# Products with W1 by Strassen-Winograd on pairs of row tiles, laid between the next steps' matmuls

## The chip, the cores and the metric

The kernel runs on one core of one Trainium2 chip. The metric is the device time in microseconds (us), the median over repeated executions. All data is fp32.

## What is computed

There are 3327 rows (26 tiles of 128, the last one padded) with 512 columns; `adj` is 3327 x 3327. With h = relu(layernorm(x)):

```python
# layer 0: attention, a bias of twice the adjacency
q = h @ Wq.T + bq;  k = h @ Wk.T + bk;  v = h @ Wv.T + bv
a = q @ k.T * scale + adj + adj
x = x + softmax(a) @ v
# layer 1: normalised graph convolution, h made again from the new x
A2 = adj + eye;  d = diagonal(A2) ** -0.5
temp = A2 @ h @ W1.T
x = x + relu((d[:, None] * A2 * d[None, :]) @ temp)
```

The products with W1 that the title speaks of are `(A2 @ h) @ W1.T`, 26 tiles of 128 x 512 by 512 x 512, each scaled by d.

## The kernel before

After the scores (lines up to about 570) the kernel does three large products one after the other, which the code numbers g = 0, 1, 2: softmax weights times h, A2 times h, A2 times temp. Each is a 2 x 2 Winograd scheme of seven products, taken in the order `ORDER` = p5, p1, p6, p7, p2, p3, p4. Each of the seven is done for two strips of output columns (s = 0, 896 wide, and s = 1, 768 wide), and each of these is a second Winograd level along the 13 row tiles: six steps t = 0 to 5 of a pair of tiles, seven matmuls each into seven PSUM banks, and one step t = None for the thirteenth tile, four matmuls. There are 294 steps; step k = ((g * 7 + place in ORDER) * 2 + s) * 7 + t. A matmul of a step has 448 columns for s = 0 and 384 for s = 1.

`run(k)` writes the instructions of step k for all engines, in an order that is kept on each engine (`in_order` covers VectorE, TensorE, GpSimd, ScalarE and SyncE):

- SyncE: `load` of step k + 3, the left operand (L701), into a ring of five slots.
- TensorE: the seven matmuls (L782), or the four of t = None (L774).
- VectorE, after them: the sums of the left operand of step k + 2 (`sums`, with `four_sums`, L173 to L175, and additions on the diagonal, L764), into a ring of three slots.
- At t = 5, `Gather.first` (L810 to L814) reads four of the seven banks. At t = None, `Gather.rest` (L827 to L830) reads the other three and one more, and `Gather.settle` (L836 to L843) puts the result into the output regions `cts`. The next step, t = 0, starts over in the same banks.
- Last, what the table `between` lists for step k: `Right.load` for a right operand five steps ahead (L721), `Right.make` three steps ahead (L742 to L748 and `four_differences`, L180 to L183), and row work.

Row work follows a product once the rows of its output are complete. For g = 0 it is `attend`. For g = 1 it is `temp(i)`, one row tile in each step from k = 177 on, leaving out the steps t = None, to k = 206: four matmuls of 512 columns with W1 into bank 3 (L874, `times_weights`), a multiplication by d on ScalarE (L902), a store through GpSimd (L903). The rows are stored in DRAM and loaded back as the right operand of g = 2. For g = 2 it is `finish`: four transposes (L927), relu (L929), the addition of x (L930) and the store (L92); the x comes by `finish_load`, which ScalarE issues (L910) at the end of the step before. In the table `within`, other `finish` calls come after the fourth matmul of a step.

Of the kernel before, what the change touches and what calls it, by code (L numbers as in the profile page):

```python
# [10 lines left out]
F32 = mybir.dt.float32  # L11
AF = mybir.ActivationFunctionType
ALU = mybir.AluOpType
AX = mybir.AxisListType

P = 128
# [20 lines left out]
PAIRS = 6  # L37
# [6 lines left out]
ROW = tuple(STRIPS[s] + y * HT[s] + k for y in range(2) for s in range(2) for k in range(HT[s]))  # L44
# [3 lines left out]
def graph_layers_kernel(  # L48
# [54 lines left out]
    def mid(k, shape, name):  # L103
        return arena.tile(shape, F32, name=name, tag=f"mid{k}")

    def half(k, shape, name):
        return arena.tile(shape, F32, name=name, tag=f"half{k}")

    def bank(k, name):
        return banks.tile([P, BW], F32, name=name, tag=f"bank{k}")  # L110

    def ring(*slots):

        turn = itertools.cycle(slots)
# [23 lines left out]
    const = ctx.enter_context(tc.tile_pool(name="const", bufs=1))  # L138
# [31 lines left out]

    def four_sums(o, g):

        nc.vector.tensor_add(o[:, 0:2], g[:, 0:4:3], g[:, 1:2].to_broadcast([P, 2, g.shape[-1]]))  # L173
        nc.vector.tensor_add(o[:, 2], o[:, 1], g[:, 0])  # L174
        nc.vector.tensor_add(o[:, 3], o[:, 2], g[:, 2])  # L175

    def four_differences(b, first=0):

        if first == 0:
            yield nc.vector.tensor_sub(b[4], b[0], b[1])  # L180
        yield nc.vector.tensor_add(b[5], b[3], b[4])
        yield nc.vector.tensor_sub(b[6], b[1], b[3])
        yield nc.vector.tensor_sub(b[7], b[2], b[5])  # L183
# [47 lines left out]
    class Chain:  # L231
# [320 lines left out]
    with in_order(*(e.engine for e in (nc.vector, nc.tensor, nc.gpsimd, nc.sync))):  # L552
# [9 lines left out]
        k = len(steps)  # L562
# [75 lines left out]
    def prepared():  # L638
        nc.vector.reciprocal(rs, tot)
        nc.vector.tensor_scalar(dg, dg, 1.0, None, op0=ALU.add)  # L640
        nc.gpsimd.tensor_tensor(sd, dg, mh, op=ALU.pow)

    wv_w1 = []

    def other_weights():
        wv_w1.append(weights(w1T))


    parts = {}
# [27 lines left out]
    x_slots = [lambda k=k: view(2, 1).rearrange("p a w -> p (a w)")[:, k * D : (k + 1) * D] for k in range(3)]  # L677
    x_slots = itertools.cycle([*x_slots, lambda: mid(10, [P, D], "xt")])
    h_ring = ring((mid, 11))
    ts_ring = ring(*spare[:3])  # L680
    xr_ring = ring(*spare[:3], (half, 14))
    out_ring = ring((half, 12), (half, 13), *spare[3:])
    xr_last = ring(*((half, k) for k in (4, 5, 6)))
# [23 lines left out]
    class Right:  # L707
# [31 lines left out]
        def make(self):  # L739
            own, r = self.own, self.r  # L740
            if r == "p5":
                nc.vector.tensor_sub(own, self.two[:, :, 0:E], self.two[:, :, E:D])  # L742
            if r == "p6":
                nc.vector.tensor_add(own, own, self.two[:, :, 0:E])
                nc.vector.tensor_sub(own, own, self.two[:, :, E:D])
                nc.gpsimd.dma_start(self.t2[:, 0 : 2 * self.n], self.b[:, 0 : 2 * self.n])
            if r in ("p7", "p4"):
                nc.vector.tensor_sub(own, own, self.one)  # L748
            if self.n == 2:
                for _ in four_differences([self.b[:, k] for k in range(8)]):  # L750
                    pass

    class Step:

# [6 lines left out]

        def sums(self):
            for a, d in self.diagonals:
                nc.vector.tensor_add(a, a, d)  # L764
            if self.t is None:
                return
            self.o = o_ring3()[:, :, : Q[self.s]]
            four_sums(self.o, self.a.rearrange("p k y w -> p (k y) w"))

        def multiply(self, ps):  # L770
            a, b, w = self.a, self.right.b, Q[self.s]
# [15 lines left out]
    class Gather:  # L787
# [44 lines left out]
        def settle(self):  # L832
            r11, r12, r21, r22 = self.regions
            for k, to in enumerate(self.to):
                if self.r == "p6":
                    nc.vector.tensor_sub(r12[k], to, r11[k])  # L836
                elif self.r == "p7":
                    nc.vector.tensor_add(r21[k], to, r12[k])
                    nc.vector.tensor_sub(r12[k], r22[k], r12[k])
                    nc.vector.tensor_sub(r22[k], r21[k], r22[k])  # L840
                elif not self.place and not self.last:
                    t = {"p2": r11, "p3": r12, "p4": r21}[self.r]
                    nc.vector.tensor_add(t[k], t[k], to)  # L843

    def where(i):

# [23 lines left out]
    def times_weights(i, w):  # L870
        s, y, k = where(i)
        ps = bank(ROLE["p8"], "p8")
        for d in range(DC):
            nc.tensor.matmul(ps, cts[s][y][d][:, k * P : (k + 1) * P], w[d], start=d == 0, stop=d == DC - 1)  # L874
        return ps
# [19 lines left out]

    normed = {}

    def temp(i):

        ps = times_weights(i, wv_w1[1])  # L900
        ts = ts_ring([P, D], "ts")
        nc.scalar.mul(ts, ps, sd[:, i : i + 1])  # L902
        nc.gpsimd.dma_start(rowd[2][i], ts)  # L903

    xrs = {}

# [57 lines left out]
    def rows(g, k, i, *z):  # L964

        if g == 0:
            at(k - 2, attend_load, i)
            at(k, attend, i)
            at(k + 1, attended, i)
        elif g == 1:  # L970
            at(k, temp, i)
        else:
            at(k - 1, finish_load, i, *z)
            at(k, finish, i, *z)

    for g in range(2):
        k = number_of(g, 5, 1, 2)
        for i in ROW:  # L980
            if steps[k].t is None:
                k += 1
            rows(g, k, i)
            k += 1
    within = {}
    for (n, s, t), its in {
# [12 lines left out]
        at(number_of(2, 6, 1, 2) + n, last_load, i)  # L999
    for k, what in ((1, totals), (2, prepare), (6, prepared), (8, judge), (9, judged)):  # L1000
        at(k, what)
    at(number_of(1, 1, 0, 4), other_weights)

    for k in range(3):
        steps[k].load()
    for what in early:
        what()
    for k in range(2):
        steps[k].sums()
    banks_of, gathers = {}, {}  # L1010

    def run(k):
        step = steps[k]
        if k + 3 < len(steps):
            steps[k + 3].load()
        if step.t == 0:
            banks_of.update(seven())
        if not cts:
            set_up()
        if step.t is None:  # L1020
            banks_of["p8"] = bank(ROLE["p1"], "p8")
        t, sums = step.t, steps[k + 2].sums if k + 2 < len(steps) else tuple
        if t == PAIRS - 1:
            gathers[step.r, step.s] = Gather(step.r, step.s, k == len(steps) - 2)
        gatherer = gathers.get((step.r, step.s))
        for j, _ in enumerate(step.multiply(banks_of)):
            if j == 3 and t == PAIRS - 1 and gatherer.last:
                gatherer.first(banks_of)
            for what, args in within.get(k, ()) if j == 3 else ():
                what(*args)  # L1030
        if t is None:
            gatherer.rest(banks_of)
        sums()
        if t == PAIRS - 1 and not gatherer.last:
            gatherer.first(banks_of)
        if t is None:
            gatherer.settle()
        for what, args in between.get(k, ()):
            what(*args)

    with in_order(*(e.engine for e in (nc.vector, nc.tensor, nc.gpsimd, nc.scalar, nc.sync))):
        for k in range(len(steps)):
# [379 lines left out]
```

## Time and profile before

| | |
|---|---|
| median of 6 runs | 2211.89 us (2209.56 to 2215.72) |
| profiled execution, its own time | 2213.65 us |
| its span, first to last instruction | 2211.8 us |
| TensorE busy | 2178.4 us (98%) |
| VectorE busy | 1627.2 us (74%) |
| ScalarE busy | 230.9 us (10%) |
| mean granted TensorE clock | 0.995 |
| matmuls with W1 and Wv together (L874) | 416 records, 189.2 us |

In the profile PE is the matmul stream of TensorE and PEld its weight loads, DVE is VectorE, ACT ScalarE, POOL GpSimd, SPq and ACTq are DMA issues of SyncE and ScalarE. An fp32 matmul shows as two records, a transpose as one. A line of a timeline has start, length, engine, source line, operation, output<-input, shape and count, and in brackets the idle time before with what ended it. The length of a run of matmuls holds the tail of the last one, so the cost of one is read from the starts. A DVE entry's start-to-start distance can be smaller than its length.

### The profile page before, as it was taken

What the parts mean: (1) busy time and instruction counts of PE and PEld (TensorE: products, weight loads), DVE (VectorE), ACT (ScalarE), POOL (GpSimd) and SP (SyncE); (2) the same over time, 40 slices, a digit from 0 to 9 for tenths busy, and PEclk for the clock granted to TensorE, in tenths of its full rate; (3) what the DMA queues carried; (4) which work ended last, traced back from release to release, by engine and by line L of the source; (5) the groups of instructions that cost most, each with busy time, mean ns of one, the idle gap of its engine ahead of it and who ended that gap; (6) DMA issues with size and microseconds to landing.
All of it is one profiled execution on the core that took longest, in us unless ns stands there. A gap on an engine that the chain in (4) does not pass through costs nothing.

```text
span 2211.8 us, 20973 instructions
## 1 busy us (share of the span) xinstructions
PE 2178.4 (98%) x6268; PEld 1168.0 (53%) x6268; DVE 1627.2 (74%) x3103; ACT 230.9 (10%) x335; POOL 357.1 (16%) x551
## 2 busy tenths in 40 slices
PE   9999999999999999999999999999999999999997
PEld 6555555455545555555454555555545555555554
DVE  6369888888877788777777778886645358777776
ACT  5311121112110000000010000000000000000011
POOL 4223333333321000001222100000000000000001
PEclk9999999999999999999999999999999999999999
DMA  8568888888969898888797899876645458765684
GB/s 286 187 218 295 295 295 285 302 283 310 358 214 327 304 376 293 274 290 310 252 310 266 312 343 351 286 267 200 215 140 191 132 185 304 236 200 186 209 299 167
DMA packets 246682, 583.68 MB, mean 264 GB/s; under 512 B 34768, under 2 KB 106270, under 8 KB 246558
## 3 DMA queue, kind: packets, MB, share of 16 engines
q1 hardware_dynamic: 192270, 399.28, 54.1%
q0 software_dynamic: 44928, 167.49, 20.0%
q10 hardware_dynamic: 9360, 15.47, 2.1%
q8 instruction: 52, 0.85, 0.2%
q14 instruction: 72, 0.59, 0.1%
HBM read 414.28 MB, written 167.85 MB: 263 GB/s over the span
## 4 chain that ended last, share of the span: by engine, by line
PE 89%; DVE 4%; DMA 3%; issue 3%; POOL 1%; SPq 0%; ACT 0%; ACTq 0%; POOLq 0%; DVEq 0%
PE p L782 52%; PE Y L454 12%; PE p L874 7%; PE Z L454 6%; PE p L774 5%; PE X L454 3%; PE Y L347 1%; DMA b<-row 1%; DVE part L173 1%; PE mm L306 1%; DMA g<-in_adjT_dram 0%; PE pt L927 0%; DVE part L174 0%; PE Z L347 0%; DMA xr<-x1d 0%
## 5 line engine op out<-in xcount | busy, mean ns | idle before, releaser
L782 PE MATMUL p<-part,b 128*128 128x448 f32 (+1 forms) x3528 | 1255.3, 514 | 6.7 <-DVE part L174 4.9
L782 PEld LDWEIGHTS p<-part,b 128*128 128x128 f32 x3528 | 669.1, 190 | 572.2 <-issue 307.8
L173 DVE TENSOR_TENSOR part<-part 128x896 f32<-128x896 f32 (+1 forms) x252 | 256.9, 1020 | 96.7 <-PE p L782 41.4
L454 PE MATMUL Y<-qt,hp 128*128 128x448 f32 (+1 forms) x832 | 308.9, 514 | 2.4 <-DVE g L458 1.5
L454 PEld LDWEIGHTS Y<-qt,hp 128*128 128x128 f32 x832 | 157.0, 190 | 138.1 <-issue 72.3
L454 PE MATMUL Z<-qt,hp 128*128 128x384 f32 (+1 forms) x416 | 162.6, 513 | 0.0
L175 DVE TENSOR_TENSOR part<-part,part 128x448 f32<-128x448 f32 (+1 forms) x219 | 129.5, 591 | 16.9 <-DVE part L174 0.9
L174 DVE TENSOR_TENSOR part<-part,part 128x448 f32<-128x448 f32 (+1 forms) x219 | 129.4, 591 | 7.4
L774 PE MATMUL p<-part,b 128*128 128x448 f32 (+1 forms) x336 | 124.2, 513 | 0.0
L874 PE MATMUL p<-w,ct 128*128 128x512 f32 x272 | 123.5, 593 | 0.5 <-DVE part L886 0.5
L454 PEld LDWEIGHTS Z<-qt,hp 128*128 128x128 f32 x416 | 78.8, 190 | 67.4 <-issue 37.2
L458 DVE SCALAR_TENSOR_TENSOR g<-g,Y 128x384 f32<-128x384 f32 (+1 forms) x156 | 91.3, 585 | 28.4 <-PE Y L454 27.4
L868 POOL DMA_DIRECT2D sum<-job x52 | 28.4, 547 | 502.8 <-DVE job L865 287.0
L811 DVE TENSOR_TENSOR part<-p,part 128x384 f32<-128x384 f32 (+1 forms) x33 | 19.3, 586 | 107.2 <-PE p L782 106.5
L774 PEld LDWEIGHTS p<-part,b 128*128 128x128 f32 x336 | 63.6, 190 | 53.8 <-issue 32.6
L810 ACT COPY part<-p 128x384 f32<-128x384 f32 (+1 forms) x33 | 16.6, 502 | 685.5 <-PE p L782 684.6
L874 PEld LDWEIGHTS p<-w,ct 128*128 128x128 f32 x272 | 51.5, 190 | 59.6 <-issue 51.9
L454 PE MATMUL X<-qt,hp 128*128 128x384 f32 (+1 forms) x208 | 81.1, 512 | 0.0
L461 ACT ACTIVATE g<-g 128x768 f32<-128x768 f32 (+1 forms) x48 | 43.0, 896 | 352.4 <-DVE g L458 299.2
L446 POOL DMA_DIRECT2D sum<-o x52 | 36.8, 708 | 220.7 <-DVE o L440 152.1
L874 PE MATMUL p<-w,part 128*128 128x512 f32 x144 | 65.7, 592 | 0.0
L92 POOL DMA_DIRECT2D out_dram<-r x30 | 16.2, 541 | 304.3 <-DVE r L930 270.0
(165 smaller groups left out, 1880.5 us busy)
## 6 DMA issues: line engine op xcount, KB each, us to landing
part<-sum SPq DMA_DIRECT2D x104, 448.0 KB, 5.0
part<-p SPq DMA_DIRECT2D x91, 448.0 KB, 6.1
part<-sum SPq DMA_DIRECT2D x104, 384.0 KB, 3.5
part<-p SPq DMA_DIRECT2D x91, 384.0 KB, 4.3
part<-in_adjT_dram SPq DMA_DIRECT2D x78, 448.0 KB, 4.7
b<-row SPq DMA_DIRECT2D x234, 128.0 KB, 4.9
part<-in_adjT_dram SPq DMA_DIRECT2D x78, 384.0 KB, 3.7
g<-in_adjT_dram SPq DMA_DIRECT2D x52, 448.0 KB, 4.5
```

Source lines behind the costliest of these rows:

```text
L173: nc.vector.tensor_add(o[:, 0:2], g[:, 0:4:3], g[:, 1:2].to_broadcast([P, 2, g.shape[-1]]))
L174: nc.vector.tensor_add(o[:, 2], o[:, 1], g[:, 0])
L175: nc.vector.tensor_add(o[:, 3], o[:, 2], g[:, 2])
L306: nc.tensor.matmul(ps[r], w_q[c // 2][:, c % 2, r * P : (r + 1) * P], w_k[c // 2][:, c % 2], start=c == 0, stop=c == DC - 1)
L446: nc.gpsimd.dma_start(self.to(sumd)[:, 0:2], self.o)
L454: nc.tensor.matmul(ps[:, :wd], h_of(self.t, name, k), qt[B[name]][:, k], start=start and k == 0, stop=k == 1, skip_group_check=True)
L458: nc.vector.scalar_tensor_tensor(a[n], a[n], 2.0, ps[:, :wd], op0=ALU.mult, op1=ALU.add if sign > 0 else ALU.subtract)
L461: nc.scalar.activation(g[1], g[1], AF.Exp, **({"bias": pad} if self.t == HALF - 1 else {}))
L774: yield nc.tensor.matmul(ps[("p2", "p3", "p4", "p8")[k]][:, :w], b[:, z], a[:, 0, y], start=k == 3, stop=True)
L782: yield nc.tensor.matmul(ps[r][:, :w], b[:, i], m, start=self.t == 0, stop=self.t == PAIRS - 1 and r in ("p1", "p5", "p6", "p7"))
L868: nc.gpsimd.dma_start(sumd[self.s][self.j][:, 2 + self.k], self.a)
L874: nc.tensor.matmul(ps, cts[s][y][d][:, k * P : (k + 1) * P], w[d], start=d == 0, stop=d == DC - 1)
```

## The change

Two row tiles are taken together as a 2 x 2 block matrix (128 rows by 256 columns each) and multiplied with W1 as 2 x 2 blocks of 256 x 256 by Winograd's seven products. Each product is two matmuls of 256 columns into one half of bank 3. The 13 pairs start two steps apart. A pair's seven products are put between the matmuls of two steps: before the first and after the second, fourth and sixth matmul of one step, and after the first, third and fifth of the next.

ScalarE takes four of the seven results out of PSUM and VectorE three. VectorE makes four sums of the pair's blocks first (eight additions of 128 columns). W1's blocks come by four DMAs in step 154 instead of step 116; their four differences are made by VectorE in steps 157 to 160, and ScalarE turns a sign in step 162.

VectorE's functions become generators that yield after each instruction. In and before steps that hold such products, the work that stood after the matmuls of a step waits in a list, and two instructions of it follow each matmul of the next step. What is left of an older step is written at the end of the step. In all other steps it follows the matmuls as before. Every `between` entry with "load" in its name now comes before the step's matmuls, in every step.

```diff
     def four_sums(o, g):
-        nc.vector.tensor_add(o[:, 0:2], g[:, 0:4:3], g[:, 1:2].to_broadcast([P, 2, g.shape[-1]]))
...
+        yield nc.vector.tensor_add(o[:, 0:2], g[:, 0:4:3], g[:, 1:2].to_broadcast([P, 2, g.shape[-1]]))
...
     def other_weights():
-        wv_w1.append(weights(w1T))
+        b11, b21, b22, t1, t2, t3 = blocks((11, 12, 13), "w1")
+        b12, t4 = (mid(k, [P, 2, E], "w1") for k in (10, 11))
+        W.extend((b11, b12, b21, b22, t1, t2, t3, t4))
+        for z in range(2):
+            for y in range(2):
+                block = w1T[z * E : (z + 1) * E, y * E : (y + 1) * E]
+                nc.sync.dma_start(W[2 * z + y], block.rearrange("(c p) e -> p c e", p=P))
+        differences.append(four_differences(W))
...
-    def temp(i):
-        ps = times_weights(i, wv_w1[1])
-        ts = ts_ring([P, D], "ts")
-        nc.scalar.mul(ts, ps, sd[:, i : i + 1])
-        nc.gpsimd.dma_start(rowd[2][i], ts)
+    PARTS = (("p2", 1, True, 0, 1), ("m1", 0, True, 0, -1), ("p5", 1, False, 3, -1), ("p6", 0, False, 1, -1),
+             ("p3", 1, False, 1, 1), ("p7", 0, False, 3, 1), ("p4", 0, False, 2, 1))
+    AFTER = ((0, 0), (0, 2), (0, 4), (0, 6), (1, 1), (1, 3), (1, 5))
+    class Temp:
...
+        def sums(self):
+            a11, a12, a21, a22 = self.blocks()
+            self.o = half(14, [P, 4, 2, P], "rows")
+            for k, x, y in ((1, a21, a22), (2, None, a11), (3, None, a12), (0, a11, a21)):
+                for c in range(2):
+                    yield nc.vector.tensor_add(self.o[:, k, c], self.o[:, {2: 1, 3: 2}[k], c] if x is None else x[c], y[c])
+        def product(self, j):
+            name, h, new, n, sign = PARTS[j]
...
+            for c in range(2):
+                a = self.o[:, {"p7": 0, "p5": 1, "p6": 2, "p3": 3}[name], c] if left is None else self.blocks()[left][c]
+                nc.tensor.matmul(ps, a, W[B[name]][:, c], start=new and c == 0, stop=c == 1, skip_group_check=True)
...
+            if name in ("p2", "p5", "p6", "p4"):
+                nc.scalar.mul(to, ps, by)
+            else:
+                nc.vector.scalar_tensor_tensor(to, ps, by, to, op0=ALU.mult, op1=ALU.add)
...
     def run(k):
...
+        for what, args in between.get(k, ()):
+            if "load" in what.__name__:
+                what(*args)
...
+        weighs = any((k, j) in inserted for j in range(7))
+        if k in sums_of and not waiting:
+            do(sums_of.pop(k)())
+        for j, _ in enumerate(itertools.chain((None,), step.multiply(banks_of))):
+            for w, n in inserted.get((k, j), ()):
+                w.product(n)
...
+            if j == 2 and k in sums_of:
+                sums = sums_of.pop(k)()
+                do(sums, 4)
+                waiting.insert(1, sums)
+            elif weighs and j > 0:
+                do(first_of(waiting), 2)
         if t is None:
+            do(first_of(waiting))
             gatherer.rest(banks_of)
-        sums()
+        added = 2 + (t is None)
+        waiting.append(steps[k + 2].sums() if k + 2 < len(steps) else iter(()))
         if t == PAIRS - 1 and not gatherer.last:
+            do(first_of(waiting))
             gatherer.first(banks_of)
         if t is None:
-            gatherer.settle()
-        for what, args in between.get(k, ()):
-            what(*args)
+            waiting.append(gatherer.settle())
+        waiting.append(flow([(what, args) for what, args in between.get(k, ()) if "load" not in what.__name__]))
+        if (k + 1, 0) not in inserted and (k + 1, 1) not in inserted:
+            do(first_of(waiting))
+        while len(waiting) > added:
+            do(waiting.pop(0))
```

More of the change, by code (lines that the diff above doesn't have):

```diff
@@ L171, in four_sums @@
     def four_sums(o, g):
-        nc.vector.tensor_add(o[:, 0:2], g[:, 0:4:3], g[:, 1:2].to_broadcast([P, 2, g.shape[-1]]))
-        nc.vector.tensor_add(o[:, 2], o[:, 1], g[:, 0])
-        nc.vector.tensor_add(o[:, 3], o[:, 2], g[:, 2])
+        yield nc.vector.tensor_add(o[:, 0:2], g[:, 0:4:3], g[:, 1:2].to_broadcast([P, 2, g.shape[-1]]))
+        yield nc.vector.tensor_add(o[:, 2], o[:, 1], g[:, 0])
+        yield nc.vector.tensor_add(o[:, 3], o[:, 2], g[:, 2])
     def four_differences(b, first=0):
@@ L641, in prepared, with difference, turn_sign @@
         nc.gpsimd.tensor_tensor(sd, dg, mh, op=ALU.pow)
+        nc.scalar.mul(nsd, sd, -1.0)
     wv_w1 = []
+    W, differences = [], []
     def other_weights():
-        wv_w1.append(weights(w1T))
+        b11, b21, b22, t1, t2, t3 = blocks((11, 12, 13), "w1")
[6 more added lines that the diff above has]
+        differences.append(four_differences(W))
+    def difference():
+        next(differences[0])
+    def turn_sign():
+        nc.scalar.mul(W[0], W[0], -1.0)
+    nsd = const.tile([P, NT], F32, name="nsd")
     parts = {}
@@ L679, in graph_layers_kernel @@
     h_ring = ring((mid, 11))
-    ts_ring = ring(*spare[:3])
+    ts_slots = [lambda k=k: view(2, 1).rearrange("p a w -> p (a w)")[:, k * D : (k + 1) * D] for k in range(3)]
+    ts_slots = itertools.cycle([*ts_slots, *(lambda k=k: mid(k, [P, D], "ts") for k in range(12, 15))])
     xr_ring = ring(*spare[:3], (half, 14))
@@ L741, in make @@
             if r == "p5":
-                nc.vector.tensor_sub(own, self.two[:, :, 0:E], self.two[:, :, E:D])
+                yield nc.vector.tensor_sub(own, self.two[:, :, 0:E], self.two[:, :, E:D])
             if r == "p6":
-                nc.vector.tensor_add(own, own, self.two[:, :, 0:E])
-                nc.vector.tensor_sub(own, own, self.two[:, :, E:D])
+                yield nc.vector.tensor_add(own, own, self.two[:, :, 0:E])
+                yield nc.vector.tensor_sub(own, own, self.two[:, :, E:D])
                 nc.gpsimd.dma_start(self.t2[:, 0 : 2 * self.n], self.b[:, 0 : 2 * self.n])
             if r in ("p7", "p4"):
-                nc.vector.tensor_sub(own, own, self.one)
+                yield nc.vector.tensor_sub(own, own, self.one)
             if self.n == 2:
-                for _ in four_differences([self.b[:, k] for k in range(8)]):
-                    pass
+                yield from four_differences([self.b[:, k] for k in range(8)])
     class Step:
@@ L763, in sums @@
             for a, d in self.diagonals:
-                nc.vector.tensor_add(a, a, d)
+                yield nc.vector.tensor_add(a, a, d)
             if self.t is None:
@@ L767, in sums @@
             self.o = o_ring3()[:, :, : Q[self.s]]
-            four_sums(self.o, self.a.rearrange("p k y w -> p (k y) w"))
+            yield from four_sums(self.o, self.a.rearrange("p k y w -> p (k y) w"))
         def multiply(self, ps):
@@ L835, in settle @@
                 if self.r == "p6":
-                    nc.vector.tensor_sub(r12[k], to, r11[k])
+                    yield nc.vector.tensor_sub(r12[k], to, r11[k])
                 elif self.r == "p7":
-                    nc.vector.tensor_add(r21[k], to, r12[k])
-                    nc.vector.tensor_sub(r12[k], r22[k], r12[k])
-                    nc.vector.tensor_sub(r22[k], r21[k], r22[k])
+                    yield nc.vector.tensor_add(r21[k], to, r12[k])
+                    yield nc.vector.tensor_sub(r12[k], r22[k], r12[k])
+                    yield nc.vector.tensor_sub(r22[k], r21[k], r22[k])
                 elif not self.place and not self.last:
                     t = {"p2": r11, "p3": r12, "p4": r21}[self.r]
-                    nc.vector.tensor_add(t[k], t[k], to)
+                    yield nc.vector.tensor_add(t[k], t[k], to)
     def where(i):
@@ L896, in graph_layers_kernel, with __init__, blocks @@
     normed = {}
-    def temp(i):
-        ps = times_weights(i, wv_w1[1])
-        ts = ts_ring([P, D], "ts")
-        nc.scalar.mul(ts, ps, sd[:, i : i + 1])
-        nc.gpsimd.dma_start(rowd[2][i], ts)
+    PARTS = (("p2", 1, True, 0, 1), ("m1", 0, True, 0, -1), ("p5", 1, False, 3, -1), ("p6", 0, False, 1, -1),
+             ("p3", 1, False, 1, 1), ("p7", 0, False, 3, 1), ("p4", 0, False, 2, 1))
+    AFTER = ((0, 0), (0, 2), (0, 4), (0, 6), (1, 1), (1, 3), (1, 5))
+    class Temp:
+        def __init__(self, *its):
+            self.its = its
+        def blocks(self):
+            return [[cts[s][y][2 * z + c][:, k * P : (k + 1) * P] for c in range(2)]
+                    for s, y, k in map(where, self.its) for z in range(2)]
+        def sums(self):
[6 more added lines that the diff above has]
+            name, h, new, n, sign = PARTS[j]
+            if j == 0:
+                self.ps = bank(ROLE["p8"], "pw").rearrange("p (k e) -> p k e", k=2)
+                self.to = [next(ts_slots)() for _ in self.its]
+            left, ps = {"m1": 0, "p2": 1, "p4": 3}.get(name), self.ps[:, h]
+            for c in range(2):
+                a = self.o[:, {"p7": 0, "p5": 1, "p6": 2, "p3": 3}[name], c] if left is None else self.blocks()[left][c]
+                nc.tensor.matmul(ps, a, W[B[name]][:, c], start=new and c == 0, stop=c == 1, skip_group_check=True)
+            i = self.its[n // 2]
+            to, by = self.to[n // 2][:, n % 2 * E : (n % 2 + 1) * E], (sd if sign > 0 else nsd)[:, i : i + 1]
+            if name in ("p2", "p5", "p6", "p4"):
+                nc.scalar.mul(to, ps, by)
+            else:
+                nc.vector.scalar_tensor_tensor(to, ps, by, to, op0=ALU.mult, op1=ALU.add)
+            if j == len(PARTS) - 1:
+                for i, ts in zip(self.its, self.to):
+                    nc.gpsimd.dma_start(rowd[2][i], ts)
     xrs = {}
@@ L969, in rows @@
             at(k + 1, attended, i)
-        elif g == 1:
-            at(k, temp, i)
         else:
@@ L974, in rows @@
             at(k, finish, i, *z)
[L978 to L983, printed above, removed]
-            k += 1
+    k = number_of(0, 5, 1, 2)
+    for i in ROW:
+        if steps[k].t is None:
+            k += 1
+        rows(0, k, i)
+        k += 1
+    inserted, sums_of = {}, {}
+    k = number_of(1, 5, 1, 2)
+    for n in range(0, NT, 2):
+        if steps[k].t is None:
+            k += 1
+        w = Temp(*ROW[n : n + 2])
+        sums_of[k] = w.sums
+        for j, (later, m) in enumerate(AFTER):
+            inserted.setdefault((k + later, m), []).append((w, j))
+        k += 2
     within = {}
@@ L1001, in graph_layers_kernel @@
         at(k, what)
-    at(number_of(1, 1, 0, 4), other_weights)
+    k = number_of(1, 4, 0, 0)
+    at(k, other_weights)
+    for n in range(4):
+        at(k + 3 + n, difference)
+    at(k + 8, turn_sign)
     for k in range(3):
@@ L1006, in graph_layers_kernel, with flow, first_of, do @@
     for what in early:
-        what()
+        for _ in what() or ():
+            pass
     for k in range(2):
-        steps[k].sums()
+        for _ in steps[k].sums():
+            pass
     banks_of, gathers = {}, {}
+    waiting = []
+    def flow(tasks):
+        for what, args in tasks:
+            yield from what(*args) or (None,)
+    def first_of(parts):
+        while parts:
+            for _ in parts[0]:
+                yield
+            parts.pop(0)
+    def do(part, n=None):
+        for _ in itertools.islice(part, n):
+            pass
     def run(k):
@@ L1021, in run @@
             banks_of["p8"] = bank(ROLE["p1"], "p8")
-        t, sums = step.t, steps[k + 2].sums if k + 2 < len(steps) else tuple
+        t = step.t
+        for what, args in between.get(k, ()):
+            if "load" in what.__name__:
+                what(*args)
         if t == PAIRS - 1:
@@ L1025, in run @@
         gatherer = gathers.get((step.r, step.s))
-        for j, _ in enumerate(step.multiply(banks_of)):
-            if j == 3 and t == PAIRS - 1 and gatherer.last:
+        weighs = any((k, j) in inserted for j in range(7))
[4 more added lines that the diff above has]
+                w.product(n)
+            if j == 4 and t == PAIRS - 1 and gatherer.last:
                 gatherer.first(banks_of)
-            for what, args in within.get(k, ()) if j == 3 else ():
+            for what, args in within.get(k, ()) if j == 4 else ():
                 what(*args)
+            if j == 2 and k in sums_of:
[4 more added lines that the diff above has]
+                do(first_of(waiting), 2)
         if t is None:
+            do(first_of(waiting))
             gatherer.rest(banks_of)
-        sums()
+        added = 2 + (t is None)
+        waiting.append(steps[k + 2].sums() if k + 2 < len(steps) else iter(()))
         if t == PAIRS - 1 and not gatherer.last:
+            do(first_of(waiting))
             gatherer.first(banks_of)
         if t is None:
-            gatherer.settle()
-        for what, args in between.get(k, ()):
-            what(*args)
+            waiting.append(gatherer.settle())
[4 more added lines that the diff above has]
+            do(waiting.pop(0))
     with in_order(*(e.engine for e in (nc.vector, nc.tensor, nc.gpsimd, nc.scalar, nc.sync))):
```

## The prediction

> **What bounds the kernel now.** I read the busy times first, then the matmuls with W1 in the timeline, then what TensorE waits for, then VectorE where its work moves.
>
> ```profile
> PE 2178.4 (98%) x6268; PEld 1168.0 (53%) x6268; DVE 1627.2 (74%) x3103; ACT 230.9 (10%) x335; POOL 357.1 (16%) x551
> ```
>
> TensorE bounds the kernel: all that is idle is 33 us. A change pays if it shortens the matmul stream without opening gaps in it. From the timeline, first in the stage of `temp`, then early in the kernel among transposes:
>
> ```profile
> 1560.47 4.68 PE L782 MATMUL p<-part,b 128*128 128x384 f32 x14
> 1564.98 3.60 PE L874 MATMUL p<-w,ct 128*128 128x512 f32 x8
> 1565.41 0.19 PEld L874 LDWEIGHTS p<-w,ct 128*128 128x128 f32 x1 [0.24 <-issue]
> 1568.42 4.68 PE L782 MATMUL p<-part,b 128*128 128x384 f32 x14
> ...
> 50.45 0.60 PE L327 MATMUL tp<-ident,ht 128*128 128x128 f32 x4
> 50.88 0.81 PE L347 MATMUL Y<-hp,M 128*128 128x384 f32 x2
> ```
>
> From 1564.98 to 1568.42 eight records of 512 columns (one `temp`) take 3.44 us, 0.43 each; a step of 384 columns takes 4.51 (1560.47 to 1564.98). Four transposes of 128 columns take 0.43, 0.1075 each. So cost goes with columns, and weights load behind the matmul before. From 1550 to 1790 us TensorE's waits are empty: `temp` costs its full time today.
>
> Then VectorE around the end of a product (t = 5, None, 0):
>
> ```profile
> 1577.92 0.56 DVE L811 TENSOR_TENSOR part<-p,part 128x384 f32<-128x384 f32 x1 [12.19 <-PE p L782]
> ...
> 1580.20 0.68 DVE L748 TENSOR_TENSOR b<-b,rows 128x512 f32<-128x512 f32 x1
> ...
> 1585.16 0.56 DVE L827 TENSOR_TENSOR part<-part,p 128x384 f32<-128x384 f32 x1 [3.21 <-PE p L774]
> ...
> 1587.57 0.28 DVE L764 TENSOR_TENSOR part<-part,ident 128x128 f32<-128x128 f32 x1
> 1587.88 1.09 DVE L173 TENSOR_TENSOR part<-part 128x896 f32<-128x896 f32 x1
> ```
>
> The 12.19 us of idle says that VectorE has run ahead: the sums of the step after None were done more than ten microseconds before. From starts: `first` takes 2.28 (1577.92 to 1580.20), `rest` 2.41 (1585.16 to 1587.57).
>
> **Part 1, the matmuls.** Removed: 26 tiles x 3.435 (the mean of 3.44 and the chain's 3.43) = 89.3 us. Added: 13 pairs x 7 products x 2 matmuls x 2 records = 364 records of 256 columns. No such record is in the trace; between 0.1075 at 128 and 0.4294 at 512 the line gives 0.215. 364 x 0.215 = 78.3, so -11.0 us.
>
> A rule speaks against this. The Trainium skill, "TensorE: Matmul & The Clock Gate", under "The mechanism", says that a weight load overlaps running matmuls only when it goes to another row group; under "LDWEIGHTS (loading the stationary operand)" it prices the load of 128 columns at P/1.2, 107 ns. All loads here fill all rows, so each new record would pay its load on top: 364 x 0.107 = 39 us more, and with the 11.0 saved this part would be slower by 28. The trace decides: the load at 1565.41 lies inside its neighbour's 0.43, and transposes pass at 0.1075 although their loads last 0.14. A load of 0.19 fits inside 0.215. I take 0.215.
>
> **Part 2, VectorE beside the products.** Added per pair: eight additions of 128 columns (rows L180 to L183: 0.285 long, 0.20 to 0.33 apart), about 1.9 us, and three reads of a half bank, multiplied and added, 256 columns: 0.417 is the nearest row (L333), L886 takes 0.749 at 512; I take 0.45. Together 3.2 per pair, 42 us in a stage (1557 to 1780) where VectorE is about half idle. ScalarE's four reads of 0.38 (L311) replace two of 0.687; GpSimd stores 26 tiles as before; the pair with the seventh row tile is stored after step 185 instead of 184, and SyncE loads it first at step 191. Volume is no problem; order is. Today nothing on VectorE but `Gather` waits for recent matmuls, so it runs ahead. Now each such read waits for a matmul of the current step, and everything behind it on VectorE waits too. The lead shrinks to about a step.
>
> Where is that too little? Set time 0 at the start of step 180 (t = 5, s = 1). A matmul takes 0.644 there, 0.751 in step 182, a product 0.86. TensorE: the product p7 ends at 3.66, the step at 7.10, None at 9.68; in step 182 the third product, p5, which needs a sum of blocks, is due at 9.68 + 2 x 0.86 + 4 x 0.751 = 14.4. VectorE: the read of p7 from 3.86 (0.2 after the matmul, as at L827), to 4.3; a remainder of `make`, 4.5; the diagonal and sums for step 182, 2.6, 7.1; `first` 2.28, 9.4; `make` of step 180's list 1.66 (1596.25 to 1597.91 in the timeline), 11.1; `rest` 2.41, 13.5; two instructions of step 183's sums 1.43, 14.9; the read of m1 0.45, 15.4; the first sum of the pair 0.29, 15.7. It comes 1.3 late; with 0.1 for the semaphore, 1.4 us of TensorE idle. The end at step 195 has the same chain (two sums 1.78 in place of 1.43, no diagonal before). At 188 and 202 no `make` stands between (rights are made in steps 179 to 185 and 193 to 199): 1.66 less, no stall. Elsewhere p5 is due 1.3 to 1.5 after m1 ends and its sum comes 0.2 + 0.45 + 0.29 + a second addition's 0.2 = 1.1 after: it fits, barely; 0.5 for all such pairs. Sum +3.3, ends 0 (if lists fall better) and 8.3 (all four ends 1.4, nine other pairs 0.3).
>
> Both ends also hold the PSUM question. The skill, "PSUM — Partial Sum Buffer", under "PSUM bank collisions raise a hardware error", asks that bank 3 be guarded as a whole, though products use halves. Then each product waits for the one before to be read: 0.2 + 0.45 against 1.3 of matmuls between. No row here shows it; the 1.3 covers it unless VectorE is late, and then by the same lateness.
>
> **Part 3, what is moved.** `finish_load` now comes a step earlier on ScalarE's queue. Today:
>
> ```profile
> 2111.29 0.69 DVE L930 TENSOR_TENSOR r<-r,xr 128x512 f32<-128x512 f32 x1 [3.53 <-DMA xr<-x1d]
> ...
> 2125.52 3.27 PE L782 MATMUL p<-part,b 128*128 128x448 f32 x8 [1.63 <-DVE part L827]
> ```
>
> VectorE waits for x twice (3.53 and 3.24 us, of which 1.4 and 2.0 come after relu has ended), is late with `rest`, and TensorE waits 1.63. A load issued 5 us earlier lands in time: -1.6, ends -1.9 and 0 (another wait in its place: its slot is free only when an earlier L930 is done, and relu queues behind the load).
>
> The other loads keep their order on SyncE among themselves; it waits there for slots anyway: no cost, some tenths if a load got late. W1's four DMAs go from SyncE's place at 1265.8 us to about 1445, where its queue stands idle to 1448.99 for a slot; 1 MB in 1 KB runs, hidden, because the left operand issued behind them (1448.99) is added only at 1463.93. W1's four differences, 0.69 each (L181 on M), are 2.8 us of VectorE in steps 157 to 160 (1460 to 1476), where the sums come 2 to 5 us ahead of their matmuls and 3.35 us of idle follow: hidden; without it up to 1 us. The sign on ScalarE, about 0.9 like L408: free.
>
> **Sum.** -11.0 + 3.3 - 1.6 = -9.3. Against the profiled execution's own 2213.65 this is 2204.3 (span about 2202.5); the median of the runs shown lies 1.8 below that execution, so 2202.5.
>
> **Rivals.**
> 1. No stall is left: the pair's work falls into the gaps. For it: VectorE is half idle here. -11.0 - 1.9: 2199.
> 2. VectorE late at every pair: +8.3 and no gain from x: -2.7, 2209; with it 2208. For it: margins of 0.2. Against: a step with its 3.5 products takes TensorE 8.3 us (5.26 + 3.5 x 0.86) and VectorE's list in it is about 5.9 (sums and diagonal 2.64, `make` 1.66, four additions 0.95, one and a half reads 0.68), so lateness is made up within a step.
> 3. Slower, by the clock. A gap can cost more than itself:
>
> ```profile
> 879.91 8.41 PE L782 MATMUL p<-part,b 128*128 128x384 f32 x20 [1.93 <-DVE part L174]
> ...
> 880.00:884.00 4.00, 4.00 (x8) 2.11 (x9) 3.83 (x6) 0.00 (x0) 0.00 (x0) 0.57 0.58 178
> ...
> 1424.00:1428.00 4.00, 4.00 (x14) 2.33 (x13) 3.83 (x6) 0.00 (x0) 0.54 (x1) 1.00 0.45 144
> ```
>
> After 1.93 us of waiting the granted clock was 0.57 over the next 4 us and 8 records passed; after a gap of 1.06 it stayed 1.00 and 14 passed: some 1.8 us extra. If the four ends stall 2 us or more, each costs 3.8, 15.2 in all, plus 2.7 at other pairs: -11.0 + 17.9 = +6.9, or 2219. It decides from 2 us per end; I reckon 1.4, and a stall hands VectorE time back.
> 4. Weight loads do not hide at 256 columns: -9.3 + 39 = +30 or 2242, nearly excluded by the transposes.
>
> **Numbers.** Forecast 0.56, rival 1 0.20, rival 2 0.18, rivals 3 and 4 0.06. The measurement tells 0.2%, 4.4 us, from no change. The forecast and rival 1 lie beyond 2207.5, of rival 2 about a third: faster 0.82; the rest of rival 2, same, 0.12; slower 0.06. The range goes from rival 1 less 2 us of spread, 2197, to rival 2's 2209.5.
>
> **What would show it.** L874 keeps only the 208 records with Wv; 364 records of 256 columns stand 0.215 apart. TensorE's waits from 1550 to 1790 name additions or reads of the pair in steps 182 and 196, 1 to 2 us each. L930 no longer waits for x and the wait at L827 is gone. It would be wrong if records of 256 columns stood 0.25 or more apart, if the clock dipped in the stage, or if TensorE waited at every pair.

## The result and the profile after

The changed kernel takes 2208.09 us (median of 16 runs, 2205.46 to 2210.67), the kernel before 2212.65 in 36 runs beside it. The ratio is 0.998 with a 95% interval of 0.9974 to 0.9987. The change gains 4.6 us, just under half of the 9.3 that were forecast. The time lies inside the interval 2197.0 to 2209.5, but the forecast's own mechanism did not produce it. The matmuls cost what was worked out, VectorE's stalls beside them were smaller, and the third part, the loads of x moved ahead, turned its sign. That the sum still fell into the interval is luck.

In the profile after, the lines have moved: the steps' matmuls are L801 (before L782), the products with W1 L954, VectorE's reads of them L960, the sums of a pair L944, `rest` L846 to L849, `finish_load` L970, the transposes, relu and addition of `finish` L987, L989 and L990. The profiled execution took 2210.79 us with a span of 2208.8, which is 2.7 above the median, so the terms read from its trace are those of one long execution; that of before took 2213.65. Line 1 of the page:

```profile
PE 2173.2 (98%) x6424; PEld 1198.4 (54%) x6424; DVE 1664.8 (75%) x3250; ACT 238.4 (11%) x363; POOL 358.8 (16%) x551
```

TensorE's busy time is only 5.2 us lower. Where the time went is read from the first matmul of the same step in both timelines (after minus before, in us):

| from step to step | gain or loss |
|---|---|
| start to 175 | -0.4 |
| 175 to 210, the stage of the pairs | -8.1 |
| 210 to 280, more half clock behind a gap at step 252 | +0.3 |
| 280 to 282, the wait at `rest` | -1.9 |
| 282 to 287, in the finishing stage | +6.3 |
| 287 to 293, two short waits behind relu | +0.9 |
| 293 to the last transpose | -0.6 |

The stage of the pairs, TensorE's timeline around the end at step 181 and, below it, some of its weight loads and of VectorE's instructions:

```profile
1584.87 1.03 PE L954 MATMUL pw<-w,ct 128*128 128x256 f32 x4
1585.73 1.67 PE L801 MATMUL p<-part,b 128*128 128x448 f32 x4
1587.24 1.03 PE L954 MATMUL pw<-w,ct 128*128 128x256 f32 x4
1588.10 1.67 PE L801 MATMUL p<-part,b 128*128 128x448 f32 x4
1590.18 1.13 PE L954 MATMUL pw<-w,rows 128*128 128x256 f32 x4 [0.41 <-DVE rows L944]
...
1587.24 0.62 PEld L954 LDWEIGHTS pw<-w,ct 128*128 128x128 f32 x3 [0.18 <-issue]
...
1586.27 0.55 DVE L846 TENSOR_TENSOR part<-part,p 128x384 f32<-128x384 f32 x1
...
1588.13 0.28 DVE L783 TENSOR_TENSOR part<-part,ident 128x128 f32<-128x128 f32 x1
...
1589.45 0.48 DVE L960 SCALAR_TENSOR_TENSOR ts<-pw,nsd,ts 128x256 f32<-128x256 f32 x1
1589.85 0.48 DVE L944 TENSOR_TENSOR rows<-ct,ct 128x128 f32<-128x128 f32 x2
```

Four records of 256 columns take 0.86 (1584.87 to 1585.73, and 1587.24 to 1588.10), 0.215 each, while three weight loads pass in 0.62 beside them. The wait at 1590.18 is the one that the timetable placed at this product, by the sum that it named (the addition from 1589.85, behind the read of m1). Counted from the starts it is 0.6: the four records from 1588.10 cost 1.5.

The finishing stage is where the gain was lost. TensorE's timeline after the end at step 279:

```profile
2127.74 0.38 PE L987 MATMUL pt<-ident,ct 128*128 128x128 f32 x2
2128.17 2.42 PE L801 MATMUL p<-part,b 128*128 128x448 f32 x6
2133.86 1.12 PE L987 MATMUL pt<-ident,ct 128*128 128x128 f32 x4 [3.27 <-ACT r L989]
```

ScalarE and its DMA issues in the same stretch:

```profile
2124.93 0.69 ACT L989 ACTIVATE r<-pt,sd 128x512 f32<-128x512 f32 x1 [5.01 <-PE pt L987]
2127.66 5.36 ACTq L970 DMA_DIRECT2D xr<-x1d  x2
2133.12 0.69 ACT L989 ACTIVATE r<-pt,sd 128x512 f32<-128x512 f32 x1 [7.51 <-DVE r L990]
```

And VectorE's additions of `finish`:

```profile
2126.95 0.69 DVE L990 TENSOR_TENSOR r<-r,xr 128x512 f32<-128x512 f32 x1
2131.98 0.68 DVE L990 TENSOR_TENSOR r<-r,xr 128x512 f32<-128x512 f32 x1
```

Read the three from the middle. At 2127.66 ScalarE begins to issue two loads of x and is done only after 5.36 us. The issue of one takes about 0.33; the rest is waiting. The first starts when the addition that frees its slot ends (2127.64), the second when the next addition ends (2132.66), 0.36 before the two are done. Relu stands behind both in ScalarE's queue. Its transposes are done at 2128.3, but it starts at 2133.12. Bank 3 is not read until then, and TensorE's next transposes wait 3.27 us for it. VectorE is late with these additions because `make`, `rest`, sums and `settle` of the end at step 279 come before them in its timeline.

Busy time by stretches of 4 us (TensorE with its records first, the granted clock third from the end), in the changed kernel and, last, at the same time in the kernel before:

```profile
2130.00:2134.00 4.00, 0.73 (x3) 0.14 (x2) 2.75 (x8) 0.69 (x1) 0.54 (x1) 0.84 0.54 189
2134.00:2138.00 4.00, 4.00 (x9) 2.36 (x10) 3.74 (x7) 0.69 (x1) 0.54 (x1) 0.50 0.59 197
...
2134.00:2138.00 4.00, 4.00 (x17) 2.23 (x16) 3.86 (x10) 0.69 (x1) 0.00 (x0) 1.00 0.97 348
```

After the gap the clock was 0.50 and nine records passed in 4 us. The gap cost 3.4 and the half clock, which lasted to 2139.5, 2.8 more: the 6.3 of the table.

### The profile page after: what moved, and what is told of

Read it like the earlier page. It is cut to its first block, busy times and chain, and to the rows that moved or that the text cites. A ratio compares the mean times of both kernels' runs of the same rounds, so it can differ in the third digit from the quotient of the medians.

```text
span 2208.8 us, 21499 instructions
## 1 busy us (share of the span) xinstructions
PE 2173.2 (98%) x6424; PEld 1198.4 (54%) x6424; DVE 1664.8 (75%) x3250; ACT 238.4 (11%) x363; POOL 358.8 (16%) x551
## 5 line engine op out<-in xcount | busy, mean ns | idle before, releaser
L801 PE MATMUL p<-part,b 128*128 128x448 f32 (+1 forms) x3528 | 1268.4, 515 | 5.0 <-DVE part L174 4.9
L801 PEld LDWEIGHTS p<-part,b 128*128 128x128 f32 x3528 | 670.4, 191 | 544.2 <-issue 287.5
L893 PE MATMUL p<-w,ct 128*128 128x512 f32 x136 | 61.8, 594 | 0.4 <-DVE part L905 0.4
L454 PEld LDWEIGHTS X<-qt,hp 128*128 128x128 f32 x208 | 39.5, 190 | 33.1 <-issue 19.3
L954 PE MATMUL pw<-w,rows 128*128 128x256 f32 x208 | 53.6, 380 | 0.8 <-DVE rows L944 0.8
```

Source lines behind the costliest of these rows:

```text
L454: nc.tensor.matmul(ps[:, :wd], h_of(self.t, name, k), qt[B[name]][:, k], start=start and k == 0, stop=k == 1, skip_group_check=True)
L801: yield nc.tensor.matmul(ps[r][:, :w], b[:, i], m, start=self.t == 0, stop=self.t == PAIRS - 1 and r in ("p1", "p5", "p6", "p7"))
L954: nc.tensor.matmul(ps, a, W[B[name]][:, c], start=new and c == 0, stop=c == 1, skip_group_check=True)
```

## Experiments

The theory: the loads of x, moved ahead of the step's matmuls, wait for one of four slots, relu waits behind them in the same queue, TensorE waits for relu. The rival: VectorE lost its lead, by the pairs or by the parts, and is late for the finishing stage wherever x is loaded.

**x_late**: the changed kernel, x loaded at the end of a step again.

```diff
+    LATE = ("finish_load", "last_load")
...
-            if "load" in what.__name__:
+            if "load" in what.__name__ and what.__name__ not in LATE:
                 what(*args)
...
-        waiting.append(flow([(what, args) for what, args in between.get(k, ()) if "load" not in what.__name__]))
+        waiting.append(flow([(what, args) for what, args in between.get(k, ()) if "load" not in what.__name__ or what.__name__ in LATE]))
```

> The changed kernel with finish_load and last_load written at the end of a step again, as before; all else as changed. Theory (the early load of x waits on ScalarE's queue for its slot, relu stands behind it, and TensorE waits for relu's bank, 3.3 us, then runs at half clock): the wait for relu from 2130 us on and the half clock behind it go (6.3 us, and 0.9 near the end), the wait for rest of 1.6 (with its edges 1.9) comes back: some 2203 to 2204, 8.5 below the kernel before. Rival (VectorE lost its lead in the stage of the pairs, or through work laid in parts, and is late for the finishing stage): x's place doesn't matter, the stall of 3 us or more stays, 2208.

Measured: 2203.0 (2199.94 to 2206.76), before beside it 2213.36; ratio 0.9954 (0.994 to 0.9968). From step 282 to 293 its trace stands where that of before does, to 0.01 us: the 7.2 us of loss are gone. The stage of the pairs is the same as in the changed kernel to 0.01. The rival falls. One thing did not come as expected: the wait at `rest` came back with 0.2 only; x landed sooner in this execution. VectorE's waits for x were these, against 3.53 and 3.24 in the kernel before:

```profile
2099.89 0.69 DVE L990 TENSOR_TENSOR r<-r,xr 128x512 f32<-128x512 f32 x1 [2.54 <-DMA xr<-x1d]
2104.77 0.69 DVE L990 TENSOR_TENSOR r<-r,xr 128x512 f32<-128x512 f32 x1 [2.53 <-DMA xr<-x1d]
```

**before_x_early**: the kernel before with this one move and nothing else.

```diff
+    EARLY = ("finish_load", "last_load")
...
+        for what, args in between.get(k, ()):
+            if what.__name__ in EARLY:
+                what(*args)
         if t == PAIRS - 1:
...
         for what, args in between.get(k, ()):
-            what(*args)
+            if what.__name__ not in EARLY:
+                what(*args)
```

> The kernel before with one part of the change alone: finish_load and last_load come ahead of a step's matmuls. Theory: the wait at rest goes (-1.9), the stall behind relu with half clock comes (+6.3, and +0.9 near the end): 4 to 5 us slower than before, about 2217. Rival (the stage of the pairs causes the lateness): nothing or -1.9, 2211 to 2212.

Measured: 2217.46 (21 runs), ratio 1.0018 (1.0012 to 1.0025): slower by 4.1, with no product changed. TensorE's waits in the last 110 us have the same entry first; below it stand the longest of these waits and the stretch of 4 us behind it:

```profile
PE pt L927 <- ACT r L929: 4.7, 3, 3.3
...
2140.85 0.65 PE L927 MATMUL pt<-ident,ct 128*128 128x128 f32 x4 [3.27 <-ACT r L929]
...
2142.00:2146.00 4.00, 4.00 (x15) 2.18 (x14) 3.79 (x9) 0.23 (x1) 0.36 (x1) 1.00 0.65 216
```

So the stall comes from this move alone. The half clock, which I had expected with it, did not come in this execution (1.00). Here the waits cost 5.5 us from step 282 to 293, 4.7 of them up to step 287, and this execution took 2214.97, 2.5 less than the median. That the slower executions had the half clock as well would fit, but no trace shows it.

**x_seven**: the changed kernel with three slots more for x.

```diff
-    xr_ring = ring(*spare[:3], (half, 14))
+    def third(k, shape, name):
+        return view(2, 1).rearrange("p a w -> p (a w)")[:, k * D : (k + 1) * D]
+
+    xr_ring = ring(*spare[:3], (half, 14), *((third, k) for k in range(3)))
```

> The changed kernel with seven slots for x in place of four (three more in space that is free by then); the loads stay early. Theory: no load waits for a slot any more, so relu is never held back: the stall and the half clock go, and the gain of 1.9 us from early loads stays: 2201 to 2202, 1.5 to 2 below the kernel with late loads. Rival (lateness of VectorE itself): unchanged, 2208.

Measured: 2201.18 (2198.92 to 2204.44), ratio 0.9947 (0.9933 to 0.9961). From step 282 to 293 it loses nothing, and the 1.9 at `rest` stays gained. ScalarE's issues no longer stretch (0.81 for two) and relu comes as soon as its transposes are done:

```profile
2123.22 0.81 ACTq L973 DMA_DIRECT2D xr<-x1d  x2
2126.66 0.69 ACT L992 ACTIVATE r<-pt,sd 128x512 f32<-128x512 f32 x1 [2.76 <-PE pt L990]
```

**x_sync**: the changed kernel, four slots, loads as early, but issued by SyncE.

```diff
-        nc.scalar.dma_start(xrs[i][:, c0:c1], x1d[i][:, c0:c1])
+        nc.sync.dma_start(xrs[i][:, c0:c1], x1d[i][:, c0:c1])
...
-            nc.scalar.dma_start(xr[:, k], x1d[i + k][:, 0:E])
+            nc.sync.dma_start(xr[:, k], x1d[i + k][:, 0:E])
```

> The changed kernel with x's loads issued by SyncE in place of ScalarE, as early as in the change, with four slots. Theory (what hurts is that relu stands behind the waiting load in one queue): the load still waits for its slot, but relu doesn't; the left operands behind it on SyncE come some 8 us later, and are needed still later: 2201 to 2203. Rival (x arrives too late, or the slot itself is what TensorE ends up waiting for): stall and half clock stay, 2207 to 2208. If the left operands become late, waits of TensorE for L174 appear: 2204 to 2207.

Measured: 2200.95, ratio 0.9955 (0.9942 to 0.9967). SyncE's DMA issues in its timeline:

```profile
2125.88 5.36 SPq L970 DMA_DIRECT2D xr<-x1d  x2
2131.33 0.38 SPq L721 DMA_DIRECT2D part<-in_adjT_dram  x1
```

And ScalarE's relu:

```profile
2126.58 0.69 ACT L989 ACTIVATE r<-pt,sd 128x512 f32<-128x512 f32 x1 [2.76 <-PE pt L987]
```

The same wait of 5.36 us is there, in the other queue. A left operand stands behind it and is needed later, so it costs nothing. What hurt was the company in the queue, not the slot by itself.

**x_five**: one slot more.

```diff
-    xr_ring = ring(*spare[:3], (half, 14))
+    xr_ring = ring(*spare[:3], (half, 14), (half, 11))
```

> The changed kernel with one slot more for x, five in place of four. In the changed kernel's trace the load that held ScalarE waited for an addition (L990) that ended at 2132.7; with five slots the same load needs the addition before, which ended at 2127.6, and relu is due at about 2128. Theory (slot, then ScalarE's queue, then bank 3): the stall of 3.3 us and the half clock are gone, 2201 to 2203. If slots only move the wait to the next load, a stall of 1 to 3 us remains: 2204 to 2207.

Measured: 2206.9 (10 runs), ratio 0.9975 (0.9966 to 0.9984). I had expected it to be enough, and it is not: the wait moved to the next step's loads, which the expectation allowed for.

```profile
2132.96 5.96 ACTq L970 DMA_DIRECT2D xr<-x1d  x2
2139.02 0.69 ACT L989 ACTIVATE r<-pt,sd 128x512 f32<-128x512 f32 x1 [7.02 <-DVE r L990]
```

I had looked one step ahead; VectorE makes up its lateness over several, and each step takes two slots.

**before_x_seven**: the kernel before with early loads and seven slots (the two edits above).

> The kernel before with x's loads ahead of a step's matmuls and seven slots, nothing else. Theory: no stall behind relu, and the wait at rest (1.6, with its edges 1.9) goes: 2211, 1 to 2 below the kernel before; in its profile L930 has no long wait for xr. If the wait at rest hung on how fast x landed in that one execution, the profile has no stall but the times equal the kernel before's: 2212 to 2213.

Measured: 2211.43 (13 runs) against 2212.73, ratio 0.9994 (0.9986 to 1.0002). In the trace the wait at `rest` is gone, 1.9 against the profile of before. In the times nothing is certain. Since x_late had most of this gain in its trace with late loads, much of the 1.9 was probably the price of a slow landing in that one execution of the kernel before.

**no_parts**: the changed kernel, VectorE's list behind the matmuls as before, all sums of a pair at the start of its first step.

```diff
-            elif weighs and j > 0:
-                do(first_of(waiting), 2)
...
-        if (k + 1, 0) not in inserted and (k + 1, 1) not in inserted:
-            do(first_of(waiting))
+        do(first_of(waiting))
```

> The changed kernel with VectorE's work not laid in parts: a step's whole list follows its matmuls, as before, in the stage of the pairs too, and all eight sums of a pair are made at the start of its first step. By the timetable settle (1.82) and one make (1.66) then stand ahead of a pair's first sum after the ends at steps 181 and 195: 3.5 us more of wait at each of the two, over 2 us in all, so the clock halves too, 1.8 each: 8 to 11 us slower than the changed kernel, 2216 to 2219. If parts are worth nothing (VectorE is half idle): as the changed kernel, 2208.

Measured: 2228.24, ratio 1.007 (1.0056 to 1.0084). It is 20 us slower than the changed kernel, twice what I expected. TensorE's waits:

```profile
PE pw L954 <- DVE ts L960: 16.1, 4, 6.3
```

I had counted two ends with 4.9 each and the clock. There were three long waits (6.3, 3.1 and 5.8) and a short one (0.9), at all four ends, and the half clock behind the three long ones: all eight sums of a pair (1.6 us), not one, stand ahead of the read of m1, so the ends at 188 and 202 are late too, though no `make` is in their way. The first of these ends is worth a look. VectorE's timeline:

```profile
1592.75 0.49 DVE L944 TENSOR_TENSOR rows<-ct,ct 128x128 f32<-128x128 f32 x2
1593.15 0.89 DVE L944 TENSOR_TENSOR rows<-rows,ct 128x128 f32<-128x128 f32 x4
1593.96 0.49 DVE L944 TENSOR_TENSOR rows<-ct 128x128 f32<-128x128 f32 x2
1594.37 0.48 DVE L960 SCALAR_TENSOR_TENSOR ts<-pw,nsd,ts 128x256 f32<-128x256 f32 x1
```

TensorE's, at the product that waits, and before it ScalarE's read of the product p2:

```profile
1584.72 0.47 ACT L958 ACTIVATE ts<-pw,sd 128x256 f32<-128x256 f32 x1 [3.89 <-PE pw L954]
...
1594.90 2.08 PE L954 MATMUL pw<-w,rows 128*128 128x256 f32 x4 [6.35 <-DVE ts L960]
```

The product p5 has its sum at 1593.24, and its own half of the bank, that of p2, was read out by 1585.19. But it starts only after the read of m1 has ended (1594.85), which lies in the other half. So in these programs the bank is guarded as a whole, and a late read of one half stops the other.

**x_seven_held**: x_seven, and no parts at two places where a read of a half bank follows.

```diff
-    inserted, sums_of = {}, {}
+    inserted, sums_of, held = {}, {}, set()
...
         sums_of[k] = w.sums
+        held.add((k + 1, 2))
+        if steps[k].t == 0:
+            held.add((k, 1))
...
-            elif weighs and j > 0:
+            elif weighs and j > 0 and (k, j) not in held:
                 do(first_of(waiting), 2)
```

> Seven slots for x as in x_seven, and VectorE's list held back at two places of the stage of the pairs: no parts after the first matmul of a pair's first step when that is a t = 0 step, none after the second matmul of a pair's second step, so that the reads of m1 and p7 come earlier. Theory of the small stalls (0.6 at each of two ends, 0.14 to 0.26 in steps 193 to 199, each with a record or two at half pace behind, because a read on VectorE comes behind two parts): they go, 1.5 to 2 us, 2199 to 2200. If later parts then come too late: waits for L174 in steps 183 or 197, as x_seven or above, 2201 to 2203.

Measured: 2200.21 (2197.41 to 2203.27), ratio 0.9948 (0.9935 to 0.9961). From step 175 to 210 its trace gains 10.2 us on before, against 8.1. TensorE's waits from 1550 to 1790 us are down to one:

```profile
PE pw L957 <- DVE ts L963: 0.2, 1, 0.2
```

The times of x_late, x_seven, x_sync and x_seven_held can't be told apart: their ratios, 0.9954, 0.9947, 0.9955 and 0.9948, lie within each other's intervals. All four beat the changed kernel and the kernel before.

## Why the prediction was half right

*Part 1, the matmuls: right.* A record of 256 columns takes 0.215 to 0.216, as the line between the rows of 128 and 512 columns gave. The rule, quoted in the prediction, that a weight load of all row groups does not overlap is not what these traces show, at 256 columns either: loads of 0.19 pass beside such records. Rival 4 falls. It had taken 0.107 for a load where the trace had 0.19, so by its own rule it should have come to 364 x 0.19, some 69 us, and not to 39.

*Part 2, VectorE beside the products: right in place, too large in size.* The stage gained 8.1 where -11.0 and +3.3 give 7.7. Stalls came at the two ends with a `make` between, 181 and 195, and at none of the others. Each was 0.6, or 0.7 with the slower record behind it, not 1.4. The term that was furthest off is `rest`: I took 2.41 from the kernel before, where its four reads follow TensorE's four matmuls. When VectorE is late they wait for nothing and take 1.86 (1586.27 to 1588.13). Other pairs lost 0.1 to 0.4 each, 1.3 in all against the 0.5 set down. no_parts shows what the order of VectorE's list is worth, together with the half clock behind the gaps, in a stage where the engine is idle for a third of the time: 20 us.

*Part 3, what is moved: wrong, and this is the step that failed.* The prediction gave -1.6 with ends of -1.9 and 0. The gain was there (-1.9 in this trace), and beside it a loss of 7.2 in this execution (5.5 in that of before_x_early, where the half clock stayed away). It named the mechanism in a bracket (the slot is free only when an earlier L930 is done, and relu queues behind the load) and then bounded it by nothing lost. The error lies in the two ends. I asked whether x would come in time, which the move improves, and not who is queued behind the load when it waits, and for how long. The trace of before had what was needed: four slots and two loads per step, so a load at the start of a step needs additions of the step before, and VectorE was up to one step late after the end of a product, with an addition of `finish` at 2124.32 right before `rest`, while its relu had ended at 2119.78:

```profile
2119.09 0.69 ACT L929 ACTIVATE r<-pt,sd 128x512 f32<-128x512 f32 x1 [3.83 <-PE pt L927]
...
2124.32 0.68 DVE L930 TENSOR_TENSOR r<-r,xr 128x512 f32<-128x512 f32 x1
2124.92 0.54 DVE L827 TENSOR_TENSOR part<-part,p 128x384 f32<-128x384 f32 x1
```

Of the other loads the prediction says that they keep their order on SyncE. It passed over those of `attend`, which ScalarE issues (L881) and which moved too. They cost nothing: after minus before is -0.36 at step 40 and -0.37 at step 120.

*The sum.* With -8.1, -1.9 and +7.2 and some tenths, the trace gives -3.5 to the last transpose, -3.0 in the span, and the medians -4.6. Without the loss of 7.2 the sum would be some 2203, near what x_late measured.

*The rivals.* Rival 2 with the gain from x named 2208, the number that was measured, but its cause did not come: the stage of the pairs lost 2.9 us beside the matmuls, not 8.3. Rival 3 had the kind of price right, a gap with a lower clock behind it, but at the wrong place: not VectorE's reads of the half banks, but relu's of bank 3.

## What to carry to other kernels

When an instruction that may wait is moved ahead in a queue, list what it now stands in front of, and follow its slot back to the instruction that frees it, at the moment when that engine is latest; an early load with too few slots is a wait for somebody else. Before adding slots, count how many the lateness spans (here five were too few and seven enough; six was not run), or put the load on a queue where nothing behind it is urgent. Reads of PSUM that hold the next matmul belong first in a busy engine's list, and the long rest in parts behind them.

## What the runs showed of the hardware

I had taken the loss after a gap as fixed by its length. It is not. The same wait of 2.53 us behind an addition of the last `settle` (step 252) was followed by some 1.7 us of loss at half clock in the changed kernel, and by none in x_late, at the same instructions. First the changed kernel, then x_late:

```profile
1982.53:1985.94 3.41, 0.88 (x4) 0.51 (x5) 3.31 (x6) 0.21 (x1) 0.00 (x0) 1.00 0.80 269
1985.94:1989.35 3.41, 3.41 (x6) 1.63 (x5) 3.31 (x9) 0.27 (x1) 0.00 (x0) 0.50 0.53 155
...
1979.67:1983.08 3.41, 2.03 (x6) 0.71 (x4) 3.31 (x5) 0.00 (x0) 0.00 (x0) 1.00 0.53 153
1983.08:1986.50 3.42, 1.71 (x6) 0.97 (x7) 3.35 (x7) 0.48 (x1) 0.00 (x0) 1.00 0.69 261
1986.50:1989.91 3.41, 3.41 (x11) 1.74 (x10) 3.31 (x9) 0.00 (x0) 0.36 (x1) 1.00 0.53 156
```

The windows are cut where they are for a reason. In each of the ten traces all changes of the granted clock lie a multiple of 3.41 us apart, so each execution can be divided into windows of 3.41 us. In the changed kernel the whole wait falls into one window, and the next runs at 0.50. In x_late the border of two windows divides it, 0.8 and 1.7, and neither is followed by a lower clock.

The same holds over all ten traces, from 60 us to the last matmul. The fifteen windows with 2.01 us or more of TensorE waits were all followed by half clock. Of eight windows with 1.87 to 1.99, four were, among them those of the gap of 1.93 at about 877 us in the profiles of before and after. No window at full clock with 1.76 or less was. So in these runs a gap costs more than itself when about 2 us of it fall into one window, and where the borders fall differs from execution to execution. This is read from traces; no run was made to test it. Part of the spread between executions of one kernel, some 5 us, can be this: of the changed kernel, the four executions with a mean granted clock of 0.996 took 2205.4 to 2206.2 us, and the five with 0.993 took 2208.4 to 2210.8.
